# Six attention softmaxes in a 12-layer decoder kernel: one Exp per tile of scores, or one Exp per head and sequence

## The chip, the cores and the metric

The kernel runs on one core of a Trainium2 chip. The metric is the device time of one execution in microseconds; the time given for a kernel is the median of its runs. Engines: PE (TensorE: matmuls and transposes), DVE (VectorE), ACT (ScalarE), POOL (GpSimd) and SP (SyncE, which issues most DMAs). Each engine works through its own queue in order; engines wait for each other by semaphores.

## What is computed

The reference is a decoder of four layers on x of shape (32, 64, 256): 32 sequences of 64 tokens, all in float32. Each layer adds to x, one after the other, an attention or state-space block (`L0_attn` to `L3_attn`), a cross attention to a context of 64 tokens per sequence (`L0_xattn` to `L3_xattn`) and a feed-forward block (`L0_ffn` to `L3_ffn`), each on the layer norm of x. Six of the twelve blocks hold a softmax over keys; `L1_attn` and `L2_attn` are state-space blocks and have none.

| block | heads | scores, before the softmax | keys |
|---|---|---|---|
| L0_attn | 32 | q.k / 8 after a rotary turn, causal | 64 |
| L0_xattn | 16 | q.k / sqrt(128), masked; rows without any valid key give 0 | 64 |
| L1_xattn | 16 | q.k / sqrt(128), q and k normed by their root mean square | 64 |
| L2_xattn | 16 | q.k / 4, two softmaxes side by side, whose outputs are added | 48 and 16 |
| L3_attn | 32 | q.k / sqrt(8) after a rotary turn, causal, 4-bit rounded projections | 64 |
| L3_xattn | 32 | q.k / sqrt(8) after a turn by positions | 64 |

In each case

```
attn = softmax(scores)          # exp(scores - max) / sum(exp(scores - max)) over the keys
out  = einsum('bhts,bhsd->bhtd', attn, v)
```

## The kernel before

The 2048 tokens are 16 tiles of 128 tokens, so a tile holds two sequences of 64. x stays in SBUF. Every block is a function for one tile (or a pair of tiles), `unit_L0_attn` and so on. The 16 tiles go through the layers in three groups of 8, 6 and 2 (`GROUPS`, line 2358). The group in hand runs its wide blocks (L0, L1_attn, L1_xattn) woven with the narrow blocks (L1_ffn from its queues, L2, L3) of the group before; the last group counts L1_ffn to its wide blocks (`body` and `weave`, lines 2384 to 2419). Group 0's L0 and L1 blocks run alone, and the last group's narrow blocks are woven with L3's experts.

Nothing of this is issued at once. The calls go to a `Recorder` (line 376), which stores each operation with its operands and finds what it depends on, down to single columns of a tile. `combine` (line 429) records a tensor_tensor that may go to DVE or POOL (only DVE once `quick` is set, before the last group's narrow blocks), and `evac` (line 752) a copy out of PSUM that may go to DVE or ACT. `Order.run` (line 575) then plays the whole program through, with a duration for each operation, and thereby writes down the order of every engine's queue: at each step it takes, over the engines, the ready operation that can start first, the older one of two that are equal, looking at up to 32 ready operations of an engine and 120 us of PE work ahead. Its durations are formulas (`duration`, line 456), and `EARLY` (line 498) is how much before its end an operation lets the next one of its engine start. For ACT they read

```
small = any(v.size() == 1 and v.n > 1 for v in views) and n > 1
...
if engine == "scalar":
    if method == "activation":
        return (0.17 if psum else 0.205) + n * 0.00083 + 0.18 * (small and psum)
...
EARLY = {"vector": 0.082, "scalar": 0.1, "gpsimd": 0.04}
```

in us, where n is the number of columns. A switch of ACT's table of functions counts 1.3 us (line 608). `issue` (line 2320) emits the operations in that order.

A tile of scores `s` is a [128 x 16 x 64] buffer: 16 slots (heads, or pairs of a head and a sequence) of 64 keys. L0_attn, L3_attn and L3_xattn have two such tiles for each tile of tokens (the loop over `u`), the others one. Before the change a softmax on `s` runs as follows.

- `shift` (line 833): DVE takes the maximum of each slot (`shift_sm`), and `combine` subtracts it, spread over the 64 keys (`L_attn_b<-L_attn_b,shift_sm`).
- one ACTIVATE on ACT takes exp(scale x s) over all 1024 columns.
- `weigh` (line 825): DVE sums each slot and takes the reciprocal (`weigh_sm`); a `combine` multiplies it in.
- `turn` (line 840): PE transposes the weights in eight 128x128 blocks (`turn_mm`), and `evac` copies them out (`turn_b`).

`heads8` (line 1778), for both L3 attentions, has no sum and no product: a column of ones beside the values makes the sum in the matmul, and the output is divided by it. It names its buffers `heads_b` and `heads_sm`. L2_xattn (line 1884) takes maxima, differences and sums for the key ranges 0:48 and 48:64 apart, with one exp over both. In L0_xattn `some` is 1 for a sequence with any valid key and multiplies the reciprocals. In the profile digits are left out of buffer names, so `L_xattn_b` covers L0_xattn, L1_xattn and L2_xattn; and as all instructions are emitted in `issue`, all carry the line 2340.

Of the kernel before, what the change touches and what calls it, by code (L numbers as in the profile page):

```python
# [21 lines left out]
AF = mybir.ActivationFunctionType  # L22
ALU = mybir.AluOpType
# [17 lines left out]
def _constants():  # L41

    f = np.float32
    r = np.arange(P)
    c = {}
    c["ident"] = np.eye(P, dtype=f)
    c["ones"] = np.ones((P, P), f)

    c["causal"] = np.where(np.arange(64)[None, :] <= (r % 64)[:, None], 0.0, NEG).astype(f)

    c["upto"] = ((r % 64)[:, None] <= np.arange(64)[None, :]).astype(f)

    c["after"] = ((r[:, None] > r[None, :]) & (r[:, None] // 64 == r[None, :] // 64)).astype(f)

    c["before"] = (r[:, None] < r[None, :]).astype(f)

    c["strip8"] = ((r[:, None] % 32) // 8 == np.arange(4)[None, :]).astype(f)
    c["strip16"] = ((r[:, None] % 32) // 16 == np.arange(2)[None, :]).astype(f)

    c["parity"] = (r[:, None] // 64 == np.arange(2)[None, :]).astype(f)  # L60

    c["unit"] = np.broadcast_to(np.eye(1, 32, dtype=f), (P, 32))
    c["iota"] = np.broadcast_to(np.arange(64, dtype=f), (P, 64))
    main = ((r % 64) < 48).astype(f)
    c["mainT"] = np.zeros((P, P), f)
    c["mainT"][0], c["mainT"][1] = main, 1 - main
    c["row"] = r[:, None].astype(f)

    at = (np.arange(NT)[:, None, None] * P + r[None, :, None]) * 6 + np.arange(6)[None, None, :] - NONE
    c["parts"] = np.transpose(at, (1, 0, 2)).reshape(P, NT * 6).astype(f)  # L70
    c["mhalf"] = np.full((P, 32), -0.5, f)

    inv = f(1.0) / f(500000.0) ** (np.arange(0, 64, 2, dtype=f) / f(64))
    ang = inv[r % 32][:, None] * np.arange(64, dtype=f)[None, :]
    co, si = np.cos(ang).astype(f), np.sin(ang).astype(f)
    c["rope0"] = np.concatenate([co, si, si, co], 1)
    inv = f(1.0) / f(10000.0) ** (np.arange(0, 8, 2, dtype=f) / f(8))
    ang = (r % 64).astype(f)[:, None] * inv[None, :]
    co, si = np.cos(ang).astype(f), np.sin(ang).astype(f)
    c["rope3"] = np.concatenate([co, co, -si, si], 1)  # L80
    at, parts, n = {}, [], 0
    for k, v in c.items():
        at[k] = (n, n + v.shape[1])
        n += v.shape[1]
        parts.append(v.astype(f))
    return np.ascontiguousarray(np.concatenate(parts, 1)), at
# [289 lines left out]
class Recorder:  # L376
# [7 lines left out]
    def add(self, ways, args, kw, group=None):  # L384

        op = Op()
        op.at, op.ways, op.args, op.kw, op.group, op.behind = len(self.ops), ways, args, kw, group, []
        out = kw["out"] if "out" in kw else args[0]
        op.outs = [out] if isinstance(out, (View, Far)) else []
        views = [v.view if isinstance(v, Rows) else v for v in [*args, *kw.values()]]  # L390
        op.ins = [v for v in views if isinstance(v, (View, Far)) and v is not out]
        op.after, op.tiles, before = [], set(), {}
        for views, write in ((op.ins, False), (op.outs, True)):
            for v in views:
                t, m = v.t, v.mask()
                lo, hi = v.p0, v.p0 + v.n
                if t.psum:
                    lo, hi = 0, P
                op.tiles.add(t)
                for kept in (t.writes, t.reads) if write else (t.writes,):  # L400
                    covered = False
                    for o, l2, h2, m2 in kept:
                        if o is not op and m & m2 and lo < h2 and l2 < hi and (group is None or o.group != group):
                            before[o.at] = True
                            covered = covered or (write and not (m2 & ~m) and lo <= l2 and h2 <= hi)
                    if covered:
                        same = lambda a: group is not None and a[0].group == group
                        kept[:] = [a for a in kept if a[3] & ~m or a[1] < lo or a[2] > hi or same(a)]
        for views, write in ((op.ins, False), (op.outs, True)):
            for v in views:  # L410
                lo, hi = (0, P) if v.t.psum else (v.p0, v.p0 + v.n)
                (v.t.writes if write else v.t.reads).append((op, lo, hi, v.mask()))
        op.waits, op.ready = len(before), 0.0
        for i in before:
            self.ops[i].after.append(op)
            if self.ops[i].group is not None:
                op.behind.append(self.ops[i])
        for t in op.tiles:
            t.left += 1
            if t.first is None:  # L420
                t.first = op.at
            t.last = op.at
        self.ops.append(op)
# [234 lines left out]
class Net:  # L658
# [163 lines left out]
            self.nc.vector.scalar_tensor_tensor(x, ps, rs, x, ALU.mult, ALU.add)  # L822


    def weigh(self, s, sums_of):

        n = s.shape[1]
        sm, r = self.sm(n), self.sm(n)
        self.nc.vector.reduce_sum(sm, sums_of, AX.X)
        self.nc.vector.reciprocal(r, sm)  # L830
        return r

    def shift(self, out, s):

        n, m = s.shape[1], s.shape[2]
        mx = self.sm(n)
        self.nc.vector.reduce_max(mx, s, AX.X)
        self.nc.combine(out, s, bc(mx, 2, m), ALU.subtract)

    def turn(self, p, n):  # L840

# [24 lines left out]
    def unit_L0_attn(self, layer, W, i):  # L866
# [53 lines left out]
        for u in range(2):  # L920

            s = self.b4(16, 64)
            for j in range(2):
                nc.vector.tensor_tensor(
                    s[:, 8 * j : 8 * j + 8], split(sc[2 * u + j], 8), bc(self.k("causal"), 1, 8), ALU.add
                )
            self.shift(s, s)
            nc.scalar.activation(s, s, AF.Exp, scale=0.125)
            r = self.weigh(s, s)
            nc.combine(s, s, bc(r, 2, 64), ALU.mult)  # L930
            ss.append(s)
        terms = []
        for u in range(2):
# [118 lines left out]
    def unit_L0_xattn(self, layer, W, i):  # L1052
# [7 lines left out]
        for a in range(2):  # L1060
# [4 lines left out]
                    self.prod(ps[:, u, :], [(wq[a][:, j + u, c * P : (c + 1) * P], hT[:, c, :]) for c in range(2)])  # L1065
                self.evac(q[:, j : j + 4, :], ps)
            qs.append(q)
        mf, add, some = self.tmp(P), self.tmp(P), self.sm(2)
        nc.vector.tensor_copy(mf, mu)
        nc.vector.tensor_scalar(add, mf, 1.0, -NEG, ALU.subtract, ALU.mult)  # L1070
        nc.vector.reduce_max(some, split(mf, 2), AX.X)
        ps = self.cross_scores(qs, lambda h, b: cT[:, b * 64 : b * 64 + 64])
        s = self.b4(16, 64)
        for j in range(2):
            nc.vector.tensor_tensor(
                s[:, 8 * j : 8 * j + 8].rearrange("p (a b) n -> p a (b n)", b=2), split(ps[j], 4), bc(add, 1, 4), ALU.add
            )
        self.shift(s, s)
        nc.scalar.activation(s, s, AF.Exp, scale=128.0**-0.5)
        r = self.weigh(s, s)  # L1080

        nc.vector.tensor_tensor(split(r, 8), split(r, 8), bc(some, 1, 8), ALU.mult)
        nc.combine(s, s, bc(r, 2, 64), ALU.mult)
        self.cross_out(i, s, cx, wo, "x0_")


# [278 lines left out]
    def unit_L1_xattn(self, layer, W, i):  # L1365
# [58 lines left out]
        for b in range(4):  # L1424
            self.transpose(pt[:, b, :], rows[:, b * P : (b + 1) * P])
        ve, rq = self.sm(4, 2, 2), self.sm(4, 2, 2)
        nc.vector.tensor_scalar(
            ve, pt.rearrange("p (a b) (m r) -> p m a b r", a=2, r=32)[:, :, :, :, 0], 1.0 / 128, 1e-5, ALU.mult, ALU.add
        )
        self.power(rq.rearrange("p a b c -> p (a b c)"), ve.rearrange("p a b c -> p (a b c)"))  # L1430
        ps = self.cross_scores(qs, lambda h, b: kTs[h // 8][:, h % 8, b * 64 : b * 64 + 64])
# [2 lines left out]
        for j in range(2):  # L1434
            at = slice(8 * j, 8 * j + 8)
            nc.vector.tensor_tensor(s[:, at], split(ps[j], 8), bc(rq[:, at], 2, 64), ALU.mult)
        self.shift(s, s)
        nc.scalar.activation(s, s, AF.Exp, scale=128.0**-0.5)
        r = self.weigh(s, s)
        nc.combine(s, s, bc(r, 2, 64), ALU.mult)  # L1440
        self.cross_out(i, s, cx, wo, "x1_")


# [334 lines left out]
    def heads8(self, qT, km, vb, causal=False):  # L1778
# [4 lines left out]
        for u in range(2):  # L1783
# [3 lines left out]
            for j in range(2):  # L1787
# [2 lines left out]
                    nc.vector.tensor_tensor(s[:, at], sc[2 * u + j], bc(self.k("causal"), 1, 8), ALU.add)  # L1790
                else:
                    nc.scalar.copy(s[:, at], sc[2 * u + j])
                    nc.vector.reduce_max(mx[:, at], sc[2 * u + j], AX.X)
            if causal:
                nc.vector.reduce_max(mx, s, AX.X)
            nc.combine(s, s, bc(mx, 2, 64), ALU.subtract)
            nc.scalar.activation(s, s, AF.Exp, scale=8.0**-0.5)
            ss.append(s)
        pTs = []
        for u in range(2):  # L1800
# [83 lines left out]
    def unit_L2_xattn(self, layer, W, i):  # L1884
# [38 lines left out]
        for u in range(4):  # L1923
            nc.scalar.copy(s[:, 4 * u : 4 * u + 4], sc[u])

        sums = self.sm(2, 16)
        for a, (lo, hi) in enumerate(parts):
            mx = self.sm(16)
            nc.vector.reduce_max(mx, s[:, :, lo:hi], AX.X)
            nc.combine(s[:, :, lo:hi], s[:, :, lo:hi], bc(mx, 2, hi - lo), ALU.subtract)  # L1930
        nc.scalar.activation(s, s, AF.Exp, scale=0.25)
        for a, (lo, hi) in enumerate(parts):
            nc.vector.reduce_sum(sums[:, a], s[:, :, lo:hi], AX.X)
        r, ratio, ro = self.sm(2, 16), self.sm(16), self.sm(16)
        nc.vector.reciprocal(r, sums)
        nc.vector.tensor_tensor(ratio, sums[:, 0], r[:, 1], ALU.mult)
# [114 lines left out]
    def units_L3_xattn(self, layer):  # L2051
# [4 lines left out]
        def make():  # L2056
# [17 lines left out]
            for j, (turn, add) in enumerate(((0.0, 0.0), (0.25, np.pi / 2))):  # L2074
# [7 lines left out]
                nc.vector.tensor_scalar(r, r, add, 3.141592, ALU.add, ALU.min)  # L2082
                nc.vector.tensor_single_scalar(r, r, -3.141592, ALU.max)
                nc.scalar.activation(o, r, AF.Sin)

        self.once("x3", [w, par[:, :2], *(par[:, j, :64] for j in (5, 6))], make)
        return lambda i: self.unit_L3_xattn(layer, w, par, tabs, i)
# [351 lines left out]
```

## Time and profile before

| | |
|---|---|
| median of 3 runs | 3205.41 us (3201.11 to 3210.14) |
| the profiled execution: its own time, its span | 3220.28 us, 3218.4 us |
| mean granted clock of PE | 0.963 |
| ACT, exps over 1024 columns | 144, 1057 to 1060 ns each on the mean of their groups |
| ACT, table loads | 146, 1283 ns each |
| DVE, maxima of 16 slots of 64 keys | 96, 1206 to 1211 ns each |
| DVE, sums of 16 slots of 64 keys | 64, 1205 to 1211 ns each |
| POOL, product or difference of 1024 columns | 1904 to 1937 ns each |

The profile is that of one execution; its times are counted from its first instruction. "Busy" is the time in which an engine had an instruction under way, and instructions of one engine may overlap. In lists of groups the columns are line, engine, operation, output and inputs by buffer name, shapes, count, then busy us and mean ns of one, then the idle time of the engine just before them with what ended it. In a timeline the columns are start and length in us, engine, operation, count, and in brackets the idle time before with what ended it. The row PEclk of the 40 slices is the clock that PE was granted, in tenths.

### The profile page before, as it was taken

How to read it: one execution, taken by the hardware profiler on the slowest of the kernel's cores; microseconds unless marked ns; L12 is line 12 of the kernel's file. 1: busy time of each engine (PE TensorE's matmuls, PEld its weight loads, DVE VectorE, ACT ScalarE, POOL GpSimd, SP SyncE). 2: the span in 40 equal slices, each digit the busy share in tenths (PEclk: the TensorE clock that was granted, in tenths of full speed). 3: DMA queues.
4: the chain of work that ended last, by engine and by line, in shares of the span. 5: the costliest groups of instructions: out<-in, count | busy, mean ns of one | idle time of the engine just before them, and what ended most of it. 6: DMA issues, size and time to landing. Idle time of an engine off the chain costs nothing.

```text
span 3218.4 us, 66418 instructions
## 1 busy us (share of the span) xinstructions
PE 3007.1 (93%) x26862; PEld 2378.3 (74%) x26862; DVE 2124.8 (66%) x5250; ACT 1421.4 (44%) x2643; POOL 1373.5 (43%) x1240
## 2 busy tenths in 40 slices
PE   8999999999999999999999999999999989997689
PEld 6888887777777877787777677677777767775466
DVE  5673347675456667655879986676656787776673
ACT  1233325656442333433555655554335554444341
POOL 4442142214464555225653455454634664443420
PEclk9999999999999899999989999898999999997899
DMA  4103320031431433111000010022562120222450
GB/s 153 33 28 133 110 70 1 18 126 57 177 129 49 153 124 103 50 44 61 27 32 23 2 65 21 25 83 90 177 218 76 38 89 15 69 97 88 141 189 14
DMA packets 112950, 256.99 MB, mean 80 GB/s; under 512 B 26309, under 2 KB 73688, under 8 KB 100228
## 3 DMA queue, kind: packets, MB, share of 16 engines
q1 hardware_dynamic: 97860, 204.73, 18.1%
q0 software_dynamic: 14784, 48.01, 4.4%
q8 instruction: 213, 3.49, 0.4%
q14 instruction: 93, 0.76, 0.1%
HBM read 177.34 MB, written 78.77 MB: 80 GB/s over the span
## 4 chain that ended last, share of the span: by engine, by line
PE 63%; DVE 23%; ACT 5%; POOL 4%; issue 3%; DMA 1%; SPq 0%; POOLq 0%; DVEq 0%; ACTq 0%
PE L_xattn_mm L2340 8%; PE cross_out_mm L2340 8%; PE ssm_heads_mm L2340 8%; PE L_attn_mm L2340 7%; PE pair_mm L2340 5%; DVE ssm_heads_b L2340 4%; PE L_ffn_mm L2340 4%; PE turn_mm L2340 3%; PE L_block_mm L2340 3%; PE rope_mm L2340 3%; DVE L_xattn_b L2340 2%; PE L_dense_mm L2340 2%; DVE L_attn_b L2340 2%; PE L_experts_mm L2340 2%; DVE L_xattn_sm L2340 2%
## 5 line engine op out<-in xcount | busy, mean ns | idle before, releaser
L2340 PE MATMUL pair_mm<-norm_b,load_ssm_w 128*128 128x256 f32 x1280 | 306.4, 384 | 0.3 <-DVE heads_b L2340 0.3
L2340 PEld LDWEIGHTS pair_mm<-norm_b,load_ssm_w 128*128 128x128 f32 x1280 | 236.6, 191 | 44.0 <-issue 8.2
L2340 POOL TENSOR_TENSOR norm_sm<-norm_sm,__init___consts 128x1 f32<-128x1 f32 (+1 forms) x142 | 88.1, 624 | 341.6 <-DVE norm_sm L2340 333.2
L2340 POOL TENSOR_TENSOR L_xattn_sm<-L_xattn_sm,__init___consts 128x8 f32<-128x8 f32 (+2 forms) x62 | 178.2, 2879 | 85.8 <-DVE L_xattn_sm L2340 62.0
L2340 ACT COPY turn_b<-turn_mm 128x512 f32<-128x512 f32 x237 | 130.8, 589 | 171.5 <-PE turn_mm L2340 167.5
L2340 DVE SCALAR_TENSOR_TENSOR ssm_heads_b<-pair_mm,load_ssm_wp,ssm_heads_b 128x252 f32<-128x252 f32 (+2 forms) x480 | 193.6, 465 | 11.8 <-ACT ssm_heads_b L2340 11.4
L2340 ACT ACT_TABLE_LOAD x146 | 187.3, 1283 | 10.1 <-PE ssm_heads_mm L2340 3.4
L2340 ACT COPY L_xattn_b<-L_xattn_mm 128x512 f32<-128x512 f32 x180 | 105.9, 589 | 179.9 <-PE L_xattn_mm L2340 179.3
L2340 PE MATMUL rope_mm<-norm_b,load_L_attn_w 128*128 128x128 f32 x1280 | 169.4, 289 | 5.1 <-DMA load_L_attn_w<-in_a_wk 4.8
L2340 PEld LDWEIGHTS rope_mm<-norm_b,load_L_attn_w 128*128 128x128 f32 x1280 | 159.6, 202 | 10.9 <-issue 9.2
L2340 PE MATMUL ssm_heads_mm<-load_ssm_w,ssm_heads_b 128*128 128x256 f32 x640 | 158.2, 390 | 7.1 <-POOL ssm_heads_b L2340 7.0
L2340 PEld LDWEIGHTS ssm_heads_mm<-load_ssm_w,ssm_heads_b 128*128 128x128 f32 x640 | 115.6, 190 | 44.3 <-issue 16.0
L2340 DVE TENSOR_TENSOR __init___x<-__init___x,cross_out_mm 128x256 f32<-128x256 f32 x32 | 13.4, 420 | 200.2 <-PE cross_out_mm L2340 200.2
L2340 POOL TENSOR_TENSOR ssm_heads_b<-ssm_heads_b,ssm_heads_b 128x1024 f32<-128x1024 f32 x28 | 66.9, 2388 | 183.1 <-DVE ssm_heads_b L2340 171.2
L2340 ACT COPY norm_b<-norm_mm 128x256 f32<-128x256 f32 (+1 forms) x132 | 54.9, 438 | 170.3 <-PE norm_mm L2340 166.3
L2340 PEld LDWEIGHTS L_xattn_mm<-norm_b,load_L_xattn_w 128*128 128x128 f32 x1024 | 122.3, 194 | 10.0 <-issue 7.7
L2340 PE MATMUL L_xattn_mm<-norm_b,load_L_xattn_w 128*128 128x128 f32 x1024 | 128.7, 280 | 0.8 <-DVE __init___x L2340 0.8
L2340 POOL TENSOR_TENSOR L_attn_b<-rope_b 128x256 f32<-128x256 f32 x132 | 99.4, 768 | 67.0 <-DVE rope_b L2340 53.5
L2340 DVE TENSOR_SCALAR norm_b<-__init___x,norm_sm,norm_sm 128x256 f32<-128x256 f32 x192 | 93.6, 505 | 48.2 <-POOL norm_sm L2340 39.6
L2340 PEld LDWEIGHTS cross_out_mm<-load_L_xattn_w,cross_out_b 128*128 128x128 f32 x512 | 99.7, 197 | 32.9 <-ACT cross_out_b L2340 17.2
L2340 PE MATMUL cross_out_mm<-load_L_xattn_w,cross_out_b 128*128 128x256 f32 x512 | 120.0, 394 | 4.2 <-ACT cross_out_b L2340 3.3
L2340 PE MATMUL L_xattn_mm<-norm_b,units_L_xattn_w 128*128 128x128 f32 x1024 | 120.8, 277 | 2.0 <-DVE norm_sm L2340 1.2
(438 smaller groups left out, 7874.1 us busy)
## 6 DMA issues: line engine op xcount, KB each, us to landing
queue<-far_w SPq DMA_DIRECT2D x14, 1024.0 KB, 17.0
L_block_w<-in_f_rows SPq DMA_DIRECT2D x16, 770.0 KB, 4.4
load_ssm_w<-in_s_in SPq DMA_DIRECT2D x12, 1024.0 KB, 5.3
parts<-far_w SPq DMA_DIRECT2D x10, 1024.0 KB, 16.3
slots<-far_w SPq DMA_DIRECT2D x16, 548.0 KB, 6.7
L_experts_b<-slots SPq DMA_DIRECT2D x32, 274.0 KB, 4.2
units_L_xattn_w<-kept_x SPq DMA_DIRECT2D x8, 1024.0 KB, 10.3
L_parts_b<-parts SPq DMA_DIRECT2D x14, 512.0 KB
```

Of the source, the lines that this page charges most:

```text
L2340: done = getattr(getattr(nc, e), method)(*map(real, op.args), **{k: real(v) for k, v in op.kw.items()})
```

## The change

The difference and the single exp of a tile are replaced by one ACTIVATE for each slot, 16 for a tile of 64-key slots. Each takes the negated maximum of its slot, a [128 x 1] column, as its bias: exp(scale x s + bias). The maximum's reduction yields the negated value itself. Where the sums are needed (all but L3), each ACTIVATE also writes the sum of its output as a second result (`accum_out`), and DVE's sum over the tile goes. L2_xattn has 32 such ACTIVATEs for a tile, 16 over 48 keys and 16 over 16. `Recorder.add` learns that an operation can have two outputs; `duration` is as before.

So that the bias need not be scaled, scales are moved: into the constant rotary tables for L0_attn and L3_attn, into the tables made once for L3_xattn (one more small DVE operation each), into the norm of q for L1_xattn. L0_xattn and L2_xattn scale the negated maxima in a small DVE operation. In L0_xattn `some` goes; the bias is capped at 1e28 and the sum held to at least 0.5 instead.

```diff
@@ -72,11 +72,12 @@
     ang = inv[r % 32][:, None] * np.arange(64, dtype=f)[None, :]
-    co, si = np.cos(ang).astype(f), np.sin(ang).astype(f)
+    co, si = ((g(ang.astype(float)) * 0.125**0.5).astype(f) for g in (np.cos, np.sin))
     c["rope0"] = np.concatenate([co, si, si, co], 1)
     ang = (r % 64).astype(f)[:, None] * inv[None, :]
-    co, si = np.cos(ang).astype(f), np.sin(ang).astype(f)
+    co, si = ((g(ang.astype(float)) * 8**-0.25).astype(f) for g in (np.cos, np.sin))
     c["rope3"] = np.concatenate([co, co, -si, si], 1)
@@ -386,9 +387,9 @@
         out = kw["out"] if "out" in kw else args[0]
-        op.outs = [out] if isinstance(out, (View, Far)) else []
+        op.outs = [v for v in (out, kw.get("accum_out")) if isinstance(v, (View, Far))]
         views = [v.view if isinstance(v, Rows) else v for v in [*args, *kw.values()]]
-        op.ins = [v for v in views if isinstance(v, (View, Far)) and v is not out]
+        op.ins = [v for v in views if isinstance(v, (View, Far)) and not any(v is o for o in op.outs)]
         op.after, op.tiles, before = [], set(), {}
@@ -822,20 +823,26 @@
-    def weigh(self, s, sums_of):
-
-        n = s.shape[1]
-        sm, r = self.sm(n), self.sm(n)
-        self.nc.vector.reduce_sum(sm, sums_of, AX.X)
-        self.nc.vector.reciprocal(r, sm)
-        return r
-
-    def shift(self, out, s):
-
-        n, m = s.shape[1], s.shape[2]
-        mx = self.sm(n)
-        self.nc.vector.reduce_max(mx, s, AX.X)
-        self.nc.combine(out, s, bc(mx, 2, m), ALU.subtract)
+    def exps(self, s, less, sums=None, scale=1.0):
+        for j in range(s.shape[1]):
+            at = slice(j, j + 1)
+            kw = {} if sums is None else {"accum_out": sums[:, at]}
+            self.nc.scalar.activation(s[:, j], s[:, j], AF.Exp, bias=less[:, at], scale=scale, **kw)
+    def softmax(self, s, scale=1.0, cap=None):
+        nc, n, m = self.nc, s.shape[1], s.shape[2]
+        mx, sums, r = self.sm(n), self.sm(n), self.sm(n)
+        nc.vector.reduce_max(mx, s, AX.X, negate=True)
+        if cap is not None:
+            nc.vector.tensor_scalar(mx, mx, scale, cap, ALU.mult, ALU.min)
+        self.exps(s, mx, sums, scale)
+        if cap is not None:
+            nc.vector.tensor_single_scalar(sums, sums, 0.5, ALU.max)
+        nc.vector.reciprocal(r, sums)
+        nc.combine(s, s, bc(r, 2, m), ALU.mult)
@@ -924,10 +931,7 @@
                 )
-            self.shift(s, s)
-            nc.scalar.activation(s, s, AF.Exp, scale=0.125)
-            r = self.weigh(s, s)
-            nc.combine(s, s, bc(r, 2, 64), ALU.mult)
+            self.softmax(s)
             ss.append(s)
@@ -1065,22 +1069,17 @@
             qs.append(q)
-        mf, add, some = self.tmp(P), self.tmp(P), self.sm(2)
+        mf, add = self.tmp(P), self.tmp(P)
         nc.vector.tensor_copy(mf, mu)
         nc.vector.tensor_scalar(add, mf, 1.0, -NEG, ALU.subtract, ALU.mult)
-        nc.vector.reduce_max(some, split(mf, 2), AX.X)
         ps = self.cross_scores(qs, lambda h, b: cT[:, b * 64 : b * 64 + 64])
             )
-        self.shift(s, s)
-        nc.scalar.activation(s, s, AF.Exp, scale=128.0**-0.5)
-        r = self.weigh(s, s)
-
-        nc.vector.tensor_tensor(split(r, 8), split(r, 8), bc(some, 1, 8), ALU.mult)
-        nc.combine(s, s, bc(r, 2, 64), ALU.mult)
+        self.softmax(s, 128.0**-0.5, 1.0e28)
         self.cross_out(i, s, cx, wo, "x0_")
@@ -1425,7 +1424,7 @@
         nc.vector.tensor_scalar(
-            ve, pt.rearrange("p (a b) (m r) -> p m a b r", a=2, r=32)[:, :, :, :, 0], 1.0 / 128, 1e-5, ALU.mult, ALU.add
+            ve, pt.rearrange("p (a b) (m r) -> p m a b r", a=2, r=32)[:, :, :, :, 0], 1.0, 128e-5, ALU.mult, ALU.add
         )
@@ -1434,10 +1433,7 @@
             nc.vector.tensor_tensor(s[:, at], split(ps[j], 8), bc(rq[:, at], 2, 64), ALU.mult)
-        self.shift(s, s)
-        nc.scalar.activation(s, s, AF.Exp, scale=128.0**-0.5)
-        r = self.weigh(s, s)
-        nc.combine(s, s, bc(r, 2, 64), ALU.mult)
+        self.softmax(s)
         self.cross_out(i, s, cx, wo, "x1_")
@@ -1790,11 +1786,10 @@
                     nc.scalar.copy(s[:, at], sc[2 * u + j])
-                    nc.vector.reduce_max(mx[:, at], sc[2 * u + j], AX.X)
+                    nc.vector.reduce_max(mx[:, at], sc[2 * u + j], AX.X, negate=True)
             if causal:
-                nc.vector.reduce_max(mx, s, AX.X)
-            nc.combine(s, s, bc(mx, 2, 64), ALU.subtract)
-            nc.scalar.activation(s, s, AF.Exp, scale=8.0**-0.5)
+                nc.vector.reduce_max(mx, s, AX.X, negate=True)
+            self.exps(s, mx)
             ss.append(s)
@@ -1923,14 +1918,12 @@
-        sums = self.sm(2, 16)
+        mx, sums = self.sm(2, 16), self.sm(2, 16)
         for a, (lo, hi) in enumerate(parts):
-            mx = self.sm(16)
-            nc.vector.reduce_max(mx, s[:, :, lo:hi], AX.X)
-            nc.combine(s[:, :, lo:hi], s[:, :, lo:hi], bc(mx, 2, hi - lo), ALU.subtract)
-        nc.scalar.activation(s, s, AF.Exp, scale=0.25)
+            nc.vector.reduce_max(mx[:, a], s[:, :, lo:hi], AX.X, negate=True)
+        nc.vector.tensor_scalar_mul(mx, mx, 0.25)
         for a, (lo, hi) in enumerate(parts):
-            nc.vector.reduce_sum(sums[:, a], s[:, :, lo:hi], AX.X)
+            self.exps(s[:, :, lo:hi], mx[:, a], sums[:, a], 0.25)
         r, ratio, ro = self.sm(2, 16), self.sm(16), self.sm(16)
@@ -2082,6 +2075,7 @@
                 nc.scalar.activation(o, r, AF.Sin)
+                nc.vector.tensor_scalar_mul(o, o, 8**-0.25)
```

## The prediction

> **What bounds the kernel now.** I read the page first: its busy times and slices.
>
> ```profile
> PE 3007.1 (93%) x26862; PEld 2378.3 (74%) x26862; DVE 2124.8 (66%) x5250; ACT 1421.4 (44%) x2643; POOL 1373.5 (43%) x1240
> ...
> PE   8999999999999999999999999999999989997689
> ...
> ACT  1233325656442333433555655554335554444341
> ...
> PEclk9999999999999899999989999898999999997899
> ```
>
> TensorE is busy nearly throughout; ScalarE has more than half its time free. The change leaves every matmul alone, so it can only move the 211 us in which PE is not busy (3218.4 - 3007.1) and the time lost to a lowered clock. Windows over three stretches (PE, PEld, DVE, ACT, POOL busy, then the clock) show where those lie.
>
> ```profile
> 0.00:965.00 965.00, 929.88 (x8124) 748.40 (x8124) 546.53 (x1103) 400.51 (x700) 355.25 (x285) 1.00 0.23 86
> 965.00:2897.00 1932.00, 1819.41 (x16539) 1443.19 (x16540) 1383.08 (x3462) 904.78 (x1713) 929.00 (x862) 0.96 0.21 72
> 2897.00:3218.40 321.40, 257.78 (x2202) 186.74 (x2199) 195.17 (x686) 116.07 (x232) 89.26 (x93) 0.87 0.33 108
> ```
>
> PE is idle 35 us in the first stretch, 113 in the second, 64 in the last. Summed by releaser, PE's waits are 119 us for DVE, 24 for POOL, 54 for ACT: the most that lighter vector engines could give back is 143 us, and only part of those waits is softmax:
>
> ```profile
> PE norm_mm L2340 <- DVE norm_b L2340: 35.4, 13, 7.7
> ...
> PE turn_mm L2340 <- DVE L_xattn_b L2340: 9.9, 5, 5.1
> PE turn_mm L2340 <- POOL L_xattn_b L2340: 9.8, 13, 2.8
> ```
>
> (us, times, longest). Next, the timeline of one softmax, L0_xattn's at 312 us:
>
> ```profile
> 312.38 1.06 ACT L2340 ACTIVATE L_xattn_b<-L_xattn_b 128x1024 f32<-128x1024 f32 x1
> ...
> 313.67 1.21 DVE L2340 TENSOR_REDUCE weigh_sm<-L_xattn_b 128x16 f32<-128x1024 f32 x1
> ...
> 315.52 1.90 POOL L2340 TENSOR_TENSOR L_xattn_b<-L_xattn_b,weigh_sm 128x1024 f32<-128x1024 f32 x1 [2.54 <-DVE weigh_sm L2340]
> ...
> 317.48 1.09 PE L2340 MATMUL turn_mm<-__init___consts,L_xattn_b 128*128 128x128 f32 x8 [0.15 <-POOL L_xattn_b L2340]
> ```
>
> POOL ends at 317.42 and the transposes start at 317.48, after PE has idled. This is the line I build on. The order of every queue is written by the planner: it fills PE with other work for as long as it believes the softmax takes, then puts the transposes. So a softmax that takes longer than the planner believes stops PE for the difference, less the slack. I took that slack (last write of the weights to first transpose) for all 144 softmax tiles from the trace. Medians: 0.15 us for the 32 tiles of L0_xattn and L1_xattn, 0.26 for the 16 of L2_xattn, 0.72 for the 32 of L0_attn, 0.57 for the 64 of the L3 attentions.
>
> **What is removed.** On DVE: the sums, 32 x 1.206 + 32 x 1.210 = 77 us, and L2's half of the two rows 30.1 and 13.0, 22 us; the subtractions that DVE took, 29.2 (L3) + 7 (L0, L1) + some 12 (L2); `some` and its product, 7 us. Together some 150 us, against about 10 us of added 16-column operations. On POOL: subtractions of 85.1 + 57.0 + 55.2 + 13.4 us and part of a 15.0 row, some 215 us. On ACT: 144 exps, 66.6 + 50.7 + 33.5 = 151 us. The folded scales and the longer constant table add nothing per tile; no DMA is added or moved past a queue.
>
> **What is added.** 16 exps for each of 128 tiles and 32 for each of L2's 16: 2560 ACTIVATEs, 1536 of them with a sum. No such instruction is in the trace; these rows are nearest (busy, mean ns, then idle), with two lines of ACT's timeline:
>
> ```profile
> L2340 ACT ACTIVATE ssm_sm<-ssm_sm 128x64 f32<-128x64 f32 x16 | 4.1, 257 | 0.2
> L2340 ACT ACTIVATE norm_b<-L_ffn_sm,L_ffn_sm 128x6 f32<-128x6 f32 x13 | 3.9, 297 | 4.9 <-DVE L_ffn_sm L2340 4.8
> L2340 ACT COPY norm_b<-__init___consts 128x6 f32<-128x6 f32 x12 | 1.8, 198 | 1.4 <-PE outrows_mm L2340 1.4
> ```
> ```profile
> 2255.06 0.67 ACT L2340 ACTIVATE plan_L_ffn_rt<-L_route_sm 128x1 f32<-128x1 f32 x6
> ```
> ```profile
> 3078.89 2.01 ACT L2340 ACTIVATE heads_b<-heads_b 128x1024 f32<-128x1024 f32 x2
> ```
>
> 64 columns from SBUF take 257 ns; an operand read per partition adds 297 - 198 = 99; two exps of 1057 ns in 2.01 us overlap by about 0.10. So an exp with its bias issues every 257 + 99 - 96 = 260 ns. The second result is bounded below by nothing (it comes with the pass) and above by 297 ns (a small instruction that reads a per-partition value, not overlapped). Between them lie the one-column ACTIVATE alone, 193, and in a row, (0.67 - 0.19) / 5 = 96 ns. I take 96, the row of one-column work issued back to back. ACT then gains 2560 x 0.260 + 1536 x 0.096 = 813 us, less 151: 2083 us, 65% of the span. That fits as a total; what counts is the place.
>
> **What the planner believes.** `duration` gives an ACTIVATE from SBUF 0.205 + 64 x 0.00083 = 0.258 us whether or not its bias is a tile (line 485 charges `small` only from PSUM), and `EARLY` takes off 0.1: 0.158 per exp, and nothing for the sum. It is 0.102 short per exp and 0.198 with a sum. Per tile: L0 and L1, 16 x 0.198 = 3.17 us; L2, 32 x 0.198 = 6.34; L3, 16 x 0.102 = 1.63. For the 1024-column exp its figure, 1.055, met the measured 1.058. Queued behind the exps on ACT are PSUM copies (0.59 us each for 512 columns), whose banks PE also needs; PE meets that lateness together with the transposes', so it is counted once.
>
> Less its own slack, where that is smaller, each tile stops PE. Summed over the trace's slacks: L0_attn 62 us (26 of 32 tiles), L0/L1_xattn 82 (30 of 32), L2_xattn 87 (15 of 16), L3 51 (41 of 64), together 281 us. With the sum at nothing this is 152; at 193 ns, 417; at 297 ns, 570.
>
> Against it: the waits for DVE and POOL (143 us) shrink with 365 us less work there, and a PE that is late anyway no longer meets them. I take 130, nearly all; it cannot be much more. The clock: 1 - 0.963 of 3218 is 119 us, after 31 waits of over 1.5 us, 3.8 us each; before 965 us, waits of up to 2.4 us left it at 1.00. After 965 us there are some 40 new stops of about 3 us in L0_attn, the cross attentions and L2; I let a third of them lower it: 13 x 3.8 = 50.
>
> Sum on the profiled execution: 3220.3 + 281 - 130 + 50 = 3421. The median of the runs, 3205.4, is 15 us below that execution, so 3406; I say **3405**.
>
> The Trainium skill, ScalarE: Activation LUTs, "What ACT_TABLE_LOAD costs", gives 186 ns + 0.833 a column, 93 more for a per-partition operand and 93 of overlap: by it an exp issues every 239 ns, not 260, and the stops would be some 30 us less. TensorE: Matmul & The Clock Gate, "HAM oscillation", says that gaps under about 3.4 us leave the clock alone; this trace has lowered stretches after waits of 1.8 to 2.8 us, so the row decides; by the rule the 50 us fall away.
>
> **Rivals.**
> 1. *Faster, by relief of DVE and POOL.* If the stops are covered (ACT is free 56% of the time, and tiles of two streams are woven after 965 us), the lighter engines decide: 70 to 80% of the 143 us is won, say 100. Against it stand slacks of 0.15 to 0.7 us. It decides once slack exceeds 3 us in most L0 and L1 tiles. 3205 - 100 = **3105**.
> 2. *Within 0.3%*: PE sets the end and gain and stops cancel. **3205**.
> 3. *The sum is free.* Stops of 152, less 130, clock 10: **3237**. For it: exps and sums are one ACTIVATE in the code.
> 4. *The sum is dear*, an instruction of its own, not overlapped (193 ns): 417 - 130 + 110 (some 30 of the now longer stops lower the clock) = **3602**; at 297, 570 - 130 + 150 gives 3795. L2_xattn would then also fill ACT: its three slices from 1448 us hold 31 + 43 + 44 us of ACT, and 8 tiles x 13 us more make 222 of 241 us.
> 5. *The exps are not where it says*: the planner can place them nowhere but on ScalarE, so I give this no weight.
>
> **How the numbers follow.** Forecast 0.50, rival 3 0.12, rival 4 0.20, faster 0.14, within 0.3% 0.04. About 0.3% (10 us) is what a measurement of this kernel can tell from no change. Faster 0.14, same 0.04, slower 0.82. The range leaves out most of the faster case and the dear end of rival 4: 3180 to 3620; the forecast's own is 3300 to 3520.
>
> **What would show it.** ACT near 2080 us busy, exps at some 350 ns mean and 260 apart, with sums 350 apart (rows of their own if the sum is an instruction); DVE near 1980, POOL near 1160; PE's waits for `turn_mm` on the exps' followers up by some 280 us, in stops of 3 us in L0_xattn from 240 us on, where the clock stays 1.00. I am wrong if L0_xattn's transposes still start within 0.2 us of the planned place with PE busy before them, if the sum costs far from 96 ns, or if the new order finds PE other work.

## The result and the profile after

The changed kernel takes **3567.72 us** (median of 4 runs, 3551.93 to 3569.88) against 3203.45 (4 runs, 3201.11 to 3210.14) on the same chip: ratio 1.113, 95% interval 1.110 to 1.115. The forecast was slower by 200 us; it is slower by 364. The profiled execution took 3568.41 us, with a span of 3566.6. Its page, busy times and slices (every instruction now carries line 2334):

```profile
PE 3177.7 (89%) x26862; PEld 2469.4 (69%) x26862; DVE 2005.8 (56%) x5273; ACT 1967.0 (55%) x6472; POOL 1143.4 (32%) x1115
...
PE   8898899999999898998789999889889889997589
...
ACT  3444434656553446555666766766455677554452
...
PEclk9999999999998899998889989889999979988589
```

The matmuls are the same 26862. DVE and POOL have 119 and 230 us less to do, and none of it shows as a shorter time. The row of PE shows eights where it had nines, and PEclk falls with it. The windows below are cut where about as many matmuls are done as at the ends of the three windows of before (8101 for 8124 in the first); the first group's last unwoven block ends 84 us later than before:

```profile
0.00:1048.00 1048.00, 957.65 (x8101) 766.78 (x8102) 499.35 (x1088) 519.79 (x1638) 302.48 (x258) 0.96 0.21 78
1048.00:3200.00 2152.00, 1933.07 (x16538) 1500.91 (x16538) 1308.11 (x3499) 1286.06 (x4337) 752.30 (x764) 0.92 0.20 65
3200.00:3566.60 366.60, 286.97 (x2225) 201.70 (x2224) 198.34 (x686) 161.11 (x499) 88.62 (x93) 0.81 0.29 95
```

The clocks were 1.00, 0.96 and 0.87; ScalarE has at most 60% to do in any of the three. One L0_xattn softmax of the first group in the timeline shows what happens:

```profile
306.96 0.35 ACT L2334 ACTIVATE L_xattn_b<-L_xattn_b,softmax_sm 128x64 f32<-128x64 f32 x1
307.21 0.19 ACT L2334 ACTIVATION_READ_ACCUMULATOR L_xattn_b<-L_xattn_b,softmax_sm 128x1 f32 x1
...
307.30 0.34 ACT L2334 ACTIVATE L_xattn_b<-L_xattn_b,softmax_sm 128x64 f32<-128x64 f32 x1
...
313.03 1.90 POOL L2334 TENSOR_TENSOR L_xattn_b<-L_xattn_b,softmax_sm 128x1024 f32<-128x1024 f32 x1 [21.40 <-DVE softmax_sm L2334]
...
314.99 1.17 PE L2334 MATMUL turn_mm<-__init___consts,L_xattn_b 128*128 128x128 f32 x8 [2.64 <-POOL L_xattn_b L2334]
```

The sum is an instruction of its own; exp and sum together advance by 0.33 us (306.96 to 307.30), the planner believed 0.158. The transposes come 2.64 us after PE ran out of work. The groups give the lengths:

```profile
L2334 ACT ACTIVATE heads_b<-heads_b,heads_sm 128x64 f32<-128x64 f32 x1024 | 252.4, 340 | 7.1 <-DVE heads_sm L2334 7.0
...
L2334 ACT ACTIVATION_READ_ACCUMULATOR L_xattn_b<-L_xattn_b,softmax_sm 128x1 f32 x512 | 96.7, 189 | 0.0
```

From start to start in the trace: exp to exp 239 ns, exp to its sum 239, sum to the next exp 93. And the list of PE's waits (us, times, longest):

```profile
PE turn_mm L2334 <- POOL L_xattn_b L2334: 73.1, 22, 7.0
...
PE turn_mm L2334 <- DVE L_xattn_b L2334: 17.6, 7, 5.5
PE turn_mm L2334 <- DVE L_attn_b L2334: 11.9, 5, 2.8
```

PE's waits at `turn_mm` rose from 39.9 us to 150.6. Where the time went, from the trace: PE's idle time between its first and its last matmul rose from 200 to 378 us (+177). The time at half clock rose from 239 us in 25 periods to 575 in 72. PE was idle anyway in 35 and 112 us of it; half of what is left, 102 and 231 us, is what its work lost at half speed (+129). Together these are 307 of the 348 us that the span grew. The other 41 us lie in time in which PE counts as busy; the runs on L3 below show most of them.

### The profile page after: what moved, and what is told of

It is laid out like the page before. It is cut to its first block, busy times and chain, and to the rows that moved or that the text cites. A ratio compares the mean times of both kernels' runs of the same rounds, so it can differ in the third digit from the quotient of the medians.

```text
span 3566.6 us, 70102 instructions
## 1 busy us (share of the span) xinstructions
PE 3177.7 (89%) x26862; PEld 2469.4 (69%) x26862; DVE 2005.8 (56%) x5273; ACT 1967.0 (55%) x6472; POOL 1143.4 (32%) x1115
## 5 line engine op out<-in xcount | busy, mean ns | idle before, releaser
L2334 ACT ACTIVATE heads_b<-heads_b,heads_sm 128x64 f32<-128x64 f32 x1024 | 252.4, 340 | 7.1 <-DVE heads_sm L2334 7.0
L2334 ACT ACTIVATE L_attn_b<-L_attn_b,softmax_sm 128x64 f32<-128x64 f32 x512 | 169.9, 334 | 60.9 <-DVE softmax_sm L2334 60.8
L2334 PE MATMUL turn_mm<-__init___consts,L_xattn_b 128*128 128x128 f32 x384 | 75.8, 359 | 125.4 <-POOL L_xattn_b L2334 73.1
L2334 ACT COPY L_xattn_b<-L_xattn_mm 128x512 f32<-128x512 f32 x155 | 89.4, 585 | 160.4 <-PE L_xattn_mm L2334 160.2
L2334 ACT ACTIVATE L_xattn_b<-L_xattn_b,softmax_sm 128x64 f32<-128x64 f32 x512 | 170.3, 336 | 9.5 <-DVE softmax_sm L2334 6.8
L2334 ACT COPY turn_b<-turn_mm 128x512 f32<-128x512 f32 x192 | 108.0, 585 | 114.9 <-PE turn_mm L2334 111.9
L2334 ACT ACTIVATE L_xattn_b<-L_xattn_b,L_xattn_sm 128x16 f32<-128x16 f32 (+1 forms) x512 | 156.1, 307 | 13.2 <-DVE L_xattn_sm L2334 10.0
L2334 PEld LDWEIGHTS turn_mm<-__init___consts,L_xattn_b 128*128 128x128 f32 x384 | 61.0, 186 | 140.8 <-POOL L_xattn_b L2334 80.3
L2334 PE MATMUL turn_mm<-__init___consts,heads_b 128*128 128x128 f32 x512 | 137.5, 325 | 11.4 <-ACT heads_b L2334 2.8
L2334 PE MATMUL L_xattn_mm<-norm_b,load_L_xattn_w 128*128 128x128 f32 x1024 | 140.1, 286 | 1.6 <-ACT L_xattn_b L2334 1.6
```

What stands on the lines that cost most here:

```text
L2334: done = getattr(getattr(nc, e), method)(*map(real, op.args), **{k: real(v) for k, v in op.kw.items()})
```

## The experiments

All further runs fell on two other chips of the same kind: the misled, the told, the sums on DVE and L3 alone on one, all others on the other. The kernel before takes 3327 us on the first of these, and 3327 and 3319 us in two series on the second; so each run is compared by ratio with the kernel before in its own series. The profile of before that their traces are compared with was taken on the second of these chips, in an execution of 3333 us. The first four expectations are in us on the basis of 3205: 3240 there is a ratio of 1.011, 3400 one of 1.061. Theory A is the prediction's: the planner's shortfall stops PE, and the stops lower the clock; it has E at its side from the L3 run on. Every span is split here into PE's idle time between its first and last matmul, the clock's loss (half of the time at half clock in which PE was busy), and a rest, which is work plus the waiting that records of matmuls cover, with some 11 us before PE's first matmul and after its last:

| kernel | ratio (95%) | span | idle | clock's loss | rest | waits at `turn_mm` |
|---|---|---|---|---|---|---|
| before, first chip | | 3218 | 200 | 102 | 2916 | 40 |
| after, first chip | 1.113 (1.110 to 1.115) | 3567 | 378 | 231 | 2957 | 151 |
| before, other chip | | 3331 | 267 | 141 | 2923 | 37 |
| after | 1.0995 (1.097 to 1.102) | 3657 | 442 | 252 | 2963 | 153 |
| old kernel, planner misled | 1.038 (1.035 to 1.041) | 3443 | 357 | 166 | 2920 | 139 |
| after, planner told | 1.054 (1.052 to 1.057) | 3509 | 320 | 199 | 2990 | 67 |
| after, sums on DVE | 1.051 (1.048 to 1.054) | 3497 | 323 | 196 | 2978 | 84 |
| L3 alone | 1.040 (1.037 to 1.043) | 3443 | 260 | 192 | 2991 | 41 |
| L3 alone, told | 1.015 (1.010 to 1.019) | 3385 | 262 | 152 | 2971 | 42 |
| L3 alone, held | 1.014 (1.010 to 1.017) | 3359 | 275 | 149 | 2935 | 47 |
| L3 alone, told and held | 1.010 (1.007 to 1.013) | 3351 | 273 | 140 | 2938 | 41 |
| L2_xattn alone, told | 1.019 (1.016 to 1.021) | 3387 | 319 | 139 | 2928 | 66 |
| all six, told and held | 1.035 (1.030 to 1.040) | 3443 | 314 | 182 | 2947 | 63 |
| before, order written anew | 1.008 (1.006 to 1.011) | 3355 | 294 | 136 | 2925 | 45 |

**Before and after on another chip.** No edit.

> The kernel before, unchanged, for its profile on the same chip as the next three: chips differ (3203 us on the first, 3327 on the second). All theories: the time of the kernel before on this chip; the profile tells which waits and which clock a chip adds.

> The changed kernel, unchanged, on the same chip. All theories: a ratio of 1.11 to this chip's kernel before, with stops at the transposes above 120 us. If the ratio is nearer to 1.07, a part of the first result belongs to its chip, and the told order recovered less than it seems.

Before has a span of 3331.1 us at a mean clock of 0.943, after 3656.8 at 0.912. The waits at `turn_mm` go from 37.3 to 153.0 us, much as on the first chip, and the end of the first unwoven stretch moves from 999 to 1073 us. Idle time, clock's loss and rest grow by 175, 111 and 40 us, on the first chip by 177, 129 and 41. The loss has the same parts, on a slower base.

**The old kernel with the planner misled.** No instruction is changed. The planner is made to believe as much too little of the old softmax as it did of the new.

```diff
+        if method == "reduce_sum" and views[1].shape[1] == 16 and n >= 256:
+            return 0.082
...
         if method == "activation":
+            if args[2] == AF.Exp and not psum and n == 1024 and "scale" in kw:
+                return 0.101
```

> The kernel before with all its instructions; only its planner is told too little: 0.10 us for the 1024-column exp (measured 1.06) and 0.08 for the sums of 16 slots (measured 1.21, in L2 0.94 and 0.41). It is then 2.1 us short per softmax tile in L0 and L1, 2.2 in L2, 0.95 in L3. Theory A: stops of 133 us by the slacks of the trace before, with the clock's loss some 150 to 250 us slower, 3350 to 3450, clock near 0.94. Theory B: no instruction differs, so 3205 within 1%. Theory C: half of A, some 3300.

Measured: 1.038, under the 1.045 to 1.076 that theory A gave and over the 1.03 of theory C; theory B is out. Its waits of PE, and under them those of before from its profile on the other chip:

```profile
PE turn_mm L2344 <- POOL L_xattn_b L2344: 43.8, 20, 3.9
PE turn_mm L2344 <- ACT heads_b L2344: 33.6, 25, 5.6
...
PE turn_mm L2344 <- DVE L_attn_b L2344: 23.3, 9, 4.7
```
```profile
PE turn_mm L2340 <- DVE L_xattn_b L2340: 10.0, 6, 3.9
PE turn_mm L2340 <- POOL L_xattn_b L2340: 9.4, 13, 2.8
...
PE turn_mm L2340 <- ACT heads_b L2340: 6.1, 6, 2.8
```

A wrong belief alone, with every instruction as it was, brings 139 us of waits at `turn_mm` and 3.8%; the rest stays as before. So the shortfall suffices for a loss of this kind. It doesn't suffice for all of it: after loses 10%.

**After, with the planner told** the measured pitches.

```diff
-            return (0.17 if psum else 0.205) + n * 0.00083 + 0.18 * (small and psum)
+            t = (0.17 if psum else 0.205) + n * 0.00083 + 0.18 * (small and psum)
+            if args[2] == AF.Exp and isinstance(kw.get("bias"), View):
+                t += 0.081 + 0.093 * ("accum_out" in kw)
+            return t
```

> The changed kernel, its planner told what an exp with a tile as bias takes (81 ns more) and what the second result takes (93 ns more), the pitches measured in the changed kernel's trace. Every instruction stays; only the order may differ. Theory A (the planner's shortfall stops PE at the transposes, and the stops lower the clock): back to 3205 us or below, between 3120 and 3240, PE's waits at the transposes from 151 us to under 60, the clock at 0.96. Theory B (2560 small exps are too much or too slow on ScalarE, whatever the order): above 3450. Theory C (half of each: the longer softmax also lengthens the way through a tile): 3260 to 3400.

Measured: 1.054, within theory C's range (1.017 to 1.061) and not A's. PE's waits for the cross attentions' weights shrink from 73.1 us to

```profile
PE turn_mm L2337 <- POOL L_xattn_b L2337: 31.9, 15, 10.6
```

and in the first stretch, which is not woven, nearly everything is repaired: its end, 74 us late in after, is 4 us late; the stops before the transposes of L_xattn_b there, 16 with 38.8 us in after, become 10 with 5.3 (before had 10 with 6.1); and the time at half clock there goes from 68 to 10 us. But at the end the kernel is still 178 us behind. Theory A is shown for the unwoven stretch, and falls as the whole cause: of 9.95 points, telling gives back 4.5. The table's last columns say where to look: the rest is 67 us above before's, though the matmuls are the same, and the clock's loss is 58 us above.

**After, with the sums on DVE again**, the planner not told: `accum_out` goes, and `reduce_sum` over the tile comes back.

```diff
-        self.exps(s, mx, sums, scale)
+        self.exps(s, mx, None, scale)
+        nc.vector.reduce_sum(sums, s, AX.X)
...
```

The same is done for the two key ranges of L2_xattn.

> The changed kernel without the second results: exps per head as in the change, the sums by VectorE as before; the planner stays short by 81 ns per exp (1.3 us per tile, 2.6 in L2). Theory A: stops of 112 us in place of 234, so about half of the loss stays: 3330 to 3430. Theory B: 1536 fewer instructions on ScalarE (143 us less) but the exps stay: above 3400. Theory D (the second results alone are the loss): 3205 to 3240.

Measured: 1.051, in theory A's range (1.039 to 1.070); theories B and D are out. Without the second results, whose 93 ns the planner knows nothing of, the shortfall of a 16-exp tile falls from 2.78 to 1.30 us, and half of the loss is gone. In the first stretch the delay falls from 74 to 25 us. What stays is the exps' own shortfall and, again, a high rest. The run takes away the second results' work on ScalarE together with what the planner didn't know of it, so it doesn't tell these two apart.

**L3 alone**: the old kernel with the exps per head only in `heads8`, without sums, the planner not told.

```diff
-                nc.vector.reduce_max(mx, s, AX.X)
-            nc.combine(s, s, bc(mx, 2, 64), ALU.subtract)
-            nc.scalar.activation(s, s, AF.Exp, scale=8.0**-0.5)
+                nc.vector.reduce_max(mx, s, AX.X, negate=True)
+            for j in range(16):
+                nc.scalar.activation(s[:, j], s[:, j], AF.Exp, bias=mx[:, j : j + 1])
...
```

The scales of these two blocks move as in the change.

> The kernel before with only the two L3 attentions changed (1024 exps, no second results), planner short by 1.3 us per tile. Theory A: stops of 37 us by the slacks, with the clock some 60 us slower less what the lighter VectorE and GpSimd give: 3220 to 3280. Theory B: 40% of the exps, so 40% of the loss or more: 3350. Relief of VectorE and GpSimd (a tile's subtraction goes): below 3200.

Measured: 1.040, where theory A allowed at most 1.023. Theory B's 1.045 is nearer; the next three runs, which have the same exps, decide against it. PE isn't idle longer than before (260 us against 267) and its waits at `turn_mm` are 41 us against 37; yet the rest is 68 us larger. The timeline of this kernel at full clock shows why:

```profile
2251.14 5.10 ACT L2341 ACTIVATE heads_b<-heads_b,heads_sm 128x64 f32<-128x64 f32 x21
...
2251.76 0.33 PE L2341 MATMUL turn_mm<-__init___consts,heads_b 128*128 128x128 f32 x1 [0.56 <-ACT heads_b L2341]
...
2252.24 0.80 PE L2341 MATMUL turn_mm<-__init___consts,heads_b 128*128 128x128 f32 x2
...
2253.19 0.80 PE L2341 MATMUL turn_mm<-__init___consts,heads_b 128*128 128x128 f32 x2
```

Against it PE's timeline of before on the other chip, at full clock too:

```profile
1739.91 1.04 PE L2340 MATMUL turn_mm<-__init___consts,heads_b 128*128 128x128 f32 x8
```

Eight transposes took 1.04 us; here they come one by one, 0.477 us apart, each as soon as its two exps (2 x 0.239) are done. With one exp over the tile a transpose could not be ready before the whole tile was. Now each depends on two exps alone, so the planner, which takes what can start first, puts the transposes into PE's queue in among the exps; and as an exp takes 0.239 us and not the 0.158 believed, PE stands at the head of its queue with a 0.11 us piece of work every 0.48 us. Theory E: this drip. Of adjacent `heads_b` transposes 79 of 234 stand 0.3 to 0.7 us apart; before, 1 of 451. A transpose's record is longer than its pitch: 0.27 us in a run at full clock, where the next starts after 0.109, and 0.33 where it stands apart. So of a drip's pitch of 0.477 us, 0.33 count as busy, and the gap of 0.15 us is at the lower limit of what the lists of waits count; at half clock the record is 0.476 us, all of the pitch. Added up, PE is busy on the `heads_b` transposes 36 us longer than before (half of the time at half clock taken off), which is about half of the rest's 68; 12 us each lie at `heads_mm` and `small_scores_mm`. In after, on both chips, it is 35 or 36 of some 40.

**L3 alone with the planner told, held, and both.** Told as above. Held: the planner may not put a tile's transposes ahead of its last exp; no instruction is changed, only its order.

```diff
-        op.ins = [v for v in views if isinstance(v, (View, Far)) and v is not out]
+        op.ins = [v for v in views if isinstance(v, (View, Far)) and v is not out] + self.also
...
+            self.nc.also = [p]
             for u in range(4):
                 self.transpose(ps[:, u, :], p[:, (j + u) * P : (j + u + 1) * P])
+            self.nc.also = []
```

> Only the L3 attentions changed, the planner told the exps' 239 ns. With the planner short this was 1.040. Theory A (shortfall alone): within 1% of the kernel before. Theory E (the transposes start after the first two exps and then come one by one, one for two exps, 480 ns apart in place of 110, and PE counts as busy while it waits and has its clock lowered): telling spreads other work between them, but they still drip: 1.015 to 1.03.

> Only the L3 attentions changed, the planner still short by 1.3 us per tile, but the transposes of a tile are put in the order only after its last exp, so that they come in one run. Theory E: the pitch of the transposes back to 110 ns, most of the 4.0% gone: 1.005 to 1.02, PE's busy time near 3055 us in place of 3172. Theory A: PE stops whole, once per tile, for the same shortfall: 1.03 to 1.04 still.

> Only the L3 attentions changed, the planner told and the transposes held until the last exp. Theories A and E: nothing is left but the 4 us that a tile's exps take on ScalarE in place of 1, hidden: 0.995 to 1.012. Theory C (a tile's longer way itself is the loss): 1.02 to 1.03.

Measured: 1.015 told, 1.014 held, 1.010 with both, against 1.040. Theory E allowed each of these (told at the very edge of its range); theory A is out for told (within 1%) and for held (1.03 to 1.04), theory C for both together. Pairs of transposes at the drip's pitch fall from 79 to 7 when told (where other work now stands between most transposes), to 36 when held and to 5 with both. PE's extra busy time on these transposes goes from 36 us to 20, 9 and 2, and PE is busy 3073 us when held, for 3172 (3055 was expected). Each remedy takes most of L3's loss away with every exp in place, so theory E holds: the loss comes from where the transposes stand in PE's queue and not from the exps themselves. Of the 84 us by which holding shortens the span, 56 are the rest's and 43 the clock's, while idle time rises by 15. How the three differ can't be told: a new order alone moved the time by 0.8% (last run).

**L2_xattn alone, told.** The exps per slot only in L2_xattn, 32 for a tile; the other blocks keep one exp over the tile (with the maxima negated and the scales moved).

```diff
+    NEW = ("X2",)
...
+        if of in self.NEW:
+            self.exps(s, mx, sums if self.SUMS else None, scale)
+        else:
+            self.whole(s, mx)
+            nc.scalar.activation(s, s, AF.Exp, scale=scale)
```

> Only L2_xattn changed (32 exps with second results per tile, some 10 us of ScalarE each in place of 1), the planner told; the other softmaxes do as before. Theory C (the exps' true time on ScalarE is the loss that telling leaves, and L2_xattn's is the worst, 160 us for 16 tiles woven with other work): 2 to 3% slower, most of it between the first and the last of L2's tiles. Theory A: within 1%, as the planner knows. Theory D: 2 to 4% slower too, but spread from the first point at which the order differs.

Measured: 1.019, just under theory C's 2 to 3%, though the planner knows the lengths. The output of the first L2_xattn tile comes 10 us ahead of before (at 1501 us), that of the eighth 31 us behind (at 1706), where ScalarE does these tiles beside the wide blocks. Counted by all matmuls done, the kernel is 11 us ahead there and 11 behind, so 22 us are lost there; of the 56 us at the end another 17 come between 1950 and 2900 us, where the next six tiles lie, and 23 after that. One new order by itself lost 27 us (last run), so how much of the 56 is these tiles' isn't shown.

**All six blocks, told and held.**

> All six softmaxes as changed, the planner told and the transposes held in all of them. Told alone was 1.054. Theory E: the L3 part of that goes, 1.025 to 1.04, and what is left is L2_xattn's (1.0185 by itself). Theory A: 1.054 as before. Below 1.00 would make it a version that beats the kernel before.

Measured: 1.035, the best form of the change that was run. It is 8 us behind before at the end of the first stretch, some 100 to 112 at 1950 us, and 112 at the end: nearly the whole loss lies between 1000 and 1950 us, where the wide blocks of group 1 are woven with group 0's L2_xattn and L3. PE's waits from 1501 to 1800 us in this kernel, and under them the first of these in before on the same chip:

```profile
PE turn_mm L2364 <- POOL L_xattn_b L2364: 20.8, 5, 10.6
PE turned_mm L2364 <- POOL L_xattn_b L2364: 11.2, 4, 5.7
```
```profile
PE turn_mm L2340 <- POOL L_xattn_b L2340: 4.5, 4, 2.5
```

With true lengths the planner still finds nothing to fill these chains with. That speaks for a cost of the change itself: a softmax of 16 x 0.33 or 32 x 0.3 us on one engine, where one exp took 1.06 us. How much of the 1.035 is this and how much the luck of an order was not taken apart further.

**The old kernel with its order written anew**, by a belief of 1 ns more for a transpose.

```diff
         if method == "transpose":
-            return 0.109
+            return 0.110
```

> The kernel before, with one of the planner's durations off by a nanosecond: 0.110 us for a transpose in place of 0.109. No instruction changes, but from L1 on the queues are ordered otherwise (7254 of PE's 14788 places). Theory D (the order before is a picked one, and any other order loses): 2 to 4% slower, which would then be a part of the loss of every variant here. Theory A or C: within 1%, since the durations are as true as before; stops at the transposes as before, 40 us.

Measured: 1.008. It is within theory A's or C's 1%, and theory D is out. Still, an edit that only makes the planner write a new order can lose this much; more such orders weren't run. So of the six told or held results the differences under 1% mean nothing, and some of each loss may be this.

## Why the prediction was right and where it was wrong

The sign was right, and the mechanism in the main: the planner's shortfall stops PE. The size was not: 3405 against 3568, outside the forecast's own 3300 to 3520 too. Rival 4's 3602 lies nearer, but by luck: its price for the sum, 193 ns, is twice the measured 93.

- **What bounds the kernel.** PE, as said. But the change could move more than PE's idle time and its clock: these make up 307 of 348 us, and 41 lie in time in which PE counts as busy.
- **What is removed.** Right in amount (DVE 2006 us busy for some 1980, POOL 1143 for some 1160).
- **What is added.** An exp issues every 239 ns, not 260; the Trainium skill's figure (ScalarE: Activation LUTs, "What ACT_TABLE_LOAD costs"), which the prediction gave beside its own, is the measured one. By the trace's slacks it takes some 42 us off the stops, not the 30 stated. The second result costs 93 ns where 96 was taken, though it is an instruction of its own of 187 to 189 ns: it overlaps, so the dear rival has its premise and not its price, and the free one is out. ACT is 1967 us busy for 2083.
- **The planner's shortfall.** By the true pitches 16 x (0.332 - 0.158) = 2.78 us for a tile of L0 or L1; less 0.15 of slack 2.63. The eight stops of the first group's L0_xattn are 2.58 to 2.90 us. The misled and the told planner show that the false belief makes these stops.
- **The stops, +281.** Too large: waits at `turn_mm` rose by 111 us. The true pitches give 234; part of the remainder shows at other matmuls, where PE's waits for ACT rose from 45 to 97 us, and part in L3 as the drip, which the lists of waits hardly show. The prediction took each tile's last weights for what the transposes wait for; in L3 each waits for two exps.
- **The relief, -130.** It hardly came. Away from `turn_mm`, PE's waits for DVE and POOL went from 111 to 103 us. Both errors lie in the same idle time and nearly cancel, which is luck: 281 - 130 = 151 forecast, +177 measured.
- **The clock, +50: the step that failed.** "I let a third of them lower it: 13 x 3.8 = 50" is 47 more periods at 3.6 us each, 168 us, by the prediction's own count (one less the clock, times the span). 38 us of these fell on time in which PE was idle anyway; its work lost 129. Of the 147 us by which the span was missed (348 - 201), 79 are then the clock's, 26 idle time's, and 41 the busy time for which the sum had no term. The size of a period was about right, the number wrong. What the runs show in place of "a third" is in the next point.
- **What the stops did to the clock.** The reason given for a third, that waits of up to 2.4 us left the clock alone before 965 us, held for the single waits there, but not everywhere: in the profile of before on the other chip, the same stop of 2.4 us at 875 us is followed by 3.4 us at half clock. With each of the eight L0_xattn stops of 2.6 to 2.9 us, from 315 to 489 us, begins a stretch of 3.4 or 6.8 us at half clock, from 0.9 us before the stop's end to 1.4 after it; of all 17 stops of 2.1 to 3.2 us at the transposes in the first 1048 us, 14 are so followed and 3 are not (12 and 5 on the other chip). In the told kernel nearly all of those stops are gone, and with them the half clock (10 us of it for 68). Beyond the first stretch the link is not shown: over the whole execution 34 of the 72 periods, and 11 of 25 in before, begin so beside a stop of 1.8 us or more, and the told kernel has 539 us at half clock for 377 in before, at waits of 67 and 37 us at `turn_mm`. What starts the other periods stays open. The Trainium skill (TensorE: Matmul & The Clock Gate, "HAM oscillation") gives the rule as no idle gaps over about 3.4 us; here shorter stops too were followed by half clock, and the measurement decides.
- **What would show it.** "Stops of 3 us in L0_xattn" came; "where the clock stays 1.00" did not: 0.96.
- **Missed**: the drip, worth some 2.5 points when L3 is changed alone; and that some 3.5% stay even when the planner knows the lengths and the transposes are held, probably from L2's and the cross attentions' longer chains.

## What to carry to other kernels

Where an order is written ahead from believed durations, a new kind of instruction has first to be priced by its start-to-start pitch and told to whoever writes the order; here 0.08 to 0.17 us of false belief, 2560 times, was worth nearly half of a 10% loss. Splitting an operation also splits its dependencies: what can start early may be queued early, and then paces an engine that looks busy, so compare the rest (span less idle less the clock's loss) as well as the waits, and don't count idle time at a low clock twice. Allow for the clock beside a stop's own length: here 177 us more idle time came with 129 us lost to the clock, though only half of the periods at half clock begin at a long stop.

## What the runs showed of the hardware

- `accum_out` of an ACTIVATE becomes an ACTIVATION_READ_ACCUMULATOR of 187 to 189 ns, which adds 93 ns to the pitch of a 128x64 exp from SBUF with its bias (239 ns; 225 for 48 columns, 198 for 16).
- At half clock adjacent 128x128 transposes stand 213 ns apart, at full clock 109. Their records are longer than that, 272 ns in a run at full clock and 328 where they stand apart, so busy time hides short waits.
- Chips differ: the same program took 3203 us at a mean clock of 0.963 on the first chip, 3319 to 3327 on the others (0.943 in the profile), 3.6 to 3.9% more. The change cost 11.3% on the first and 9.95% on the one other chip where it was run unchanged.
